# A graph layer on one core: where VectorE adds a block's sums to their bins

## The chip, the core and the metric

The kernel runs on one core of a Trainium2 chip. TensorE (PE; its weight loads are PEld), VectorE (DVE), ScalarE (ACT) and GpSimd (POOL) each work through a queue of their own; SyncE (SP) starts most transfers. The metric is the device time of one execution in microseconds (us). A measurement is the median of several runs; one execution more is taken with the hardware profiler, and all rows below are of it.

## The reference

A message-passing layer over 6250 nodes and 206250 edges, sorted by destination:

```python
msg = concat([x[col], edge_attr], axis=1)          # 64 + 64 columns
h = relu(msg @ W1a.T + b1a) @ W1b.T + b1b          # 128 hidden, 64 out
sums = segment_sum(h, row, num_segments=n_nodes)   # over the edges of a node
agg = sums / maximum(counts, 1.0)[:, None]
z = relu(concat([x, agg]) @ W2a.T + b2a) @ W2b.T + b2b
out = layernorm(x + concat([z, x]) @ Wr.T + br)
```

In `reference()` the node over which a message is summed (`row`) is the edge's `src`, and the features are gathered by `dst`. The edges are sorted by `dst`, so the gather is local and the sum is not.

## The kernel before

The edges come in tiles of 128, and 13 tiles make a block; there are 124 blocks (`NGR`). For each block the kernel makes the first layer's rows, finds for each row its place in a table in DRAM that is ordered by bins of 128 nodes, and scatters the rows there with GpSimd's indirect transfers. Once tiles of the table are full they are read back and summed into their bins by matmuls with one-hot matrices. The second layer is linear, so the sums are of first-layer rows (128 columns and a count), and the second layer comes after them.

Blocks 4 to 109 are *joined*: of their tiles six (nine in some early blocks) go another way. Four edges of a bin become one row group ("quad"), and TensorE does this by matmuls with marks. The order of work on TensorE, VectorE, ScalarE and SyncE is written by hand: it is the order of the program's text, in the loop at L1763. GpSimd's queue follows the data, and its scatters of one block are paced to the next one's matmuls.

What stands in a joined block k, in the order of the text:

- `marks(k, 0)` (L1246): VectorE compares two tiles' places with all quads (L1253, 1024 elements a partition); ScalarE does a third tile in two steps (L1258, L1259). `marks(k, 1)` comes later.
- `counts_of(k + 1)` (L1108 to L1121): TensorE counts the next block's rows by bin.
- `low_bits(k)` and `hidden(k, ...)` (L1374, L1376): the direct tiles' rows, TensorE at L1383, ScalarE's ReLU at L1387.
- `sum_first(k)` (L1633): the first half of a group of sums, TensorE at L1560, into a buffer of h_ps.
- `join_bases(k + 1)` (L1127, L1131): VectorE's next work behind the counts, then `join_ranks` on TensorE (L1140 to L1152), which waits for it.
- `bins_of`, `side`, `columns`: VectorE and ScalarE work for later blocks (L1059 to L1071, L1267 to L1274, L1336).
- In every second block from 10 to 58 `nodes_ahead` (L1723): the nodes' part of the second layer, TensorE at L1727 and L1729 into h_ps, copied to nx by VectorE (L1733).
- `slots`, `join_at_slots`, the last `hidden` part, then `join(k, 0)` and `join(k, 1)` (L1278): six matmuls each (L1285) into h_ps, copied to rj by ScalarE (L1290).
- `columns(k + 2, 1)` (L1338) and `join_places` (L1174 to L1185).
- `sum_rest(k, g)` (L1646): the group's second half on TensorE, then VectorE's one-hot matrices of the next group (`mark`, L1540), then `collect(1)` (L1620).
- `join_rows(k, i)` (L1292) for both joins: two groups each of two matmuls (L1298) into one h_ps, with ScalarE's ReLU to orow behind each (L1301).

`collect(n)` takes the oldest groups out of the list `totals` until n are left, and adds each one's h_ps to `part`, the bins' sums in SBUF. VectorE does this (L1631); where the bins hold nothing yet, ScalarE copies (L1629). In a joined block `collect(1)` stands behind `totals.append(g)`, so it takes the group of the block before and leaves the block's own one.

h_ps is one pool of PSUM buffers with `bufs=5` (L768). All the matmuls named above but counts and ranks write to it, and a buffer can be written again once its reader is through. The group of sums of block k holds one from `sum_first` in block k until it is collected.

Of the kernel before, what the change touches and what calls it, by code (L numbers as in the profile page):

```python
# [488 lines left out]
def fast_path(  # L489
# [64 lines left out]
    def joined(k):  # L554
        if not JOIN_FROM <= k < JOIN_TO:
            return 0
        return 3 if k in THRICE else 2
# [206 lines left out]
    with (  # L764
# [226 lines left out]
        def join_consts():  # L991
            for g in range(QUAD):
                nc.vector.tensor_scalar(
                    quad_ramp[:, g, :], ramp, float(QUAD), BIG + g, op0=ALU.mult, op1=ALU.add
                )
            nc.vector.memset(state["steps"], QSTRIDE + FULLQUADS)
            nc.vector.memset(state["steps"][:, :1], FULLQUADS)
# [248 lines left out]
        def marks(k, i):  # L1246


            m = top.marks[(join_at[k] + i) % MARKS]
            z = z_ps[:, i * JOIN : (i + 1) * JOIN]  # L1250
            all_q = quad_ramp.rearrange("p g q -> p (g q)")
            n = JOIN - ON_ACT
            nc.vector.tensor_tensor(  # L1253
                m[:, :n, :], all_q[:, None, :].to_broadcast([P, n, QUAD * P]),
                z[:, :n, None].to_broadcast([P, n, QUAD * P]), op=ALU.is_equal,
            )
            for t in range(n, JOIN):
                nc.scalar.activation(m[:, t, :], all_q, AF.Square, bias=z_acts[k][:, i * JOIN + t : i * JOIN + t + 1], scale=-1.0)  # L1258
                nc.scalar.activation(m[:, t, :], m[:, t, :], AF.Relu, bias=ones[:, :1], scale=-1.0)  # L1259
# [360 lines left out]
        def collect(n):  # L1620

            while len(totals) > n:
                g = totals.pop(0)
                to = part[:, g.b0 : g.b0 + g.nb, :]
                bins_ = range(g.b0, g.b0 + g.nb)
                assert len({b in begun for b in bins_}) == 1
                if g.b0 not in begun:
                    begun.update(range(g.b0, g.b0 + g.nb))
                    nc.scalar.copy(to, g.ps[:, : g.nb, :])  # L1629
                else:  # L1630
                    nc.vector.tensor_add(to, to, g.ps[:, : g.nb, :])  # L1631
# [131 lines left out]
        for k, ep_ in enumerate(epoch_of):  # L1763
# [10 lines left out]
                carried(k + 2)  # L1774
            if joined(k):
                marks(k, 0)
            if k == 1:
                join_consts()
            if k == 0:
# [340 lines left out]
```

## Time and profile before

| | |
|---|---|
| median of 3 runs | 1961.84 us |
| lowest and highest | 1957.87 and 1968.04 us |
| profiled execution | 1968.19 us, of which the span of the instructions is 1966.4 us |
| granted TensorE clock, mean | 0.914 |
| sums added by VectorE (L1631) | 192, 81.2 us in all |
| sums copied by ScalarE (L1629) | 25, median 0.375 us, from 483.5 to 825.1 us |

Rows of the timeline and of the waits look like this: start in us, duration in us, engine, line, operation, `out<-in` by the program's names, count; and in square brackets the idle time of the engine ahead of it and what ended it. `remote` is a releaser that the profile can't name, `issue` a wait for nothing that it shows. In a list of waits stand the engine and line that waited, what for, and us in total, times, longest us. In a list of groups stand busy us and mean ns of one, then the idle time ahead of them in us with its releasers. TensorE's matmuls in float32 are recorded as two halves. The ends of matmuls are modelled.

### The profile page before, as it was taken

The numbers are of one execution on the slowest core, as the hardware profiler recorded it, in microseconds if no ns is written. First come the engines' busy times: TensorE is split into PE (matmuls) and PEld (weight loads), VectorE is DVE, ScalarE is ACT, GpSimd is POOL, SyncE is SP. The second block draws the span as 40 slices with busy tenths as digits, with TensorE's granted clock in tenths as the row PEclk, the third lists the DMA queues.
The fourth block names the chain that finished last, engine by engine and source line by source line (L and its number), as shares of the span: only waits on it lengthen the run. The fifth ranks groups of instructions, "written<-read, shape, count | busy, mean of one in ns | idle before, by whom it ended". The sixth has DMA issues, their size and how long they took to land.

```text
span 1966.4 us, 33425 instructions
## 1 busy us (share of the span) xinstructions
PE 1576.4 (80%) x10868; PEld 1390.9 (71%) x10868; DVE 1355.3 (69%) x2959; ACT 1116.3 (57%) x2300; POOL 1153.7 (59%) x1235
## 2 busy tenths in 40 slices
PE   5477888768888878888888788888888888888597
PEld 4356666656777767777777677767777788887596
DVE  5367777777766766777767677777777767665287
ACT  2157778766666666666766666666666633222007
POOL 5555666566665665666666666666665656666501
PEclk7678989989998999999999989999989999999699
DMA  6546676656676666756666555556565789896484
GB/s 171 155 152 204 224 226 226 225 175 210 189 218 188 193 202 199 207 168 205 180 202 191 173 167 172 182 158 196 172 198 174 209 249 270 270 276 216 115 266 113
DMA packets 248791, 387.59 MB, mean 197 GB/s; under 512 B 43573, under 2 KB 181687, under 8 KB 248607
## 3 DMA queue, kind: packets, MB, share of 16 engines
q1 hardware_dynamic: 167661, 221.23, 40.4%
q0 software_dynamic: 48048, 122.08, 17.7%
q10 hardware_dynamic: 32898, 42.05, 6.4%
q8 instruction: 89, 1.46, 0.3%
q14 instruction: 95, 0.78, 0.1%
HBM read 214.47 MB, written 170.72 MB: 196 GB/s over the span
## 4 chain that ended last, share of the span: by engine, by line
PE 51%; ACT 13%; issue 11%; DVE 10%; another core or an unknown queue 10%; DMA 3%; POOL 1%; ACTq 0%; SPq 0%; DVEq 0%; POOLq 0%
PE h_ps L1560 19%; PE h_ps L1285 10%; PE h_ps L1298 8%; PE h_ps L1383 7%; DVE marks L1253 2%; ACT marks L1258 2%; ACT orow L1387 2%; DMA rows<-orow,rowidx 2%; ACT orow L1301 2%; ACT rj L1290 1%; ACT marks L1259 1%; ACT rhs L1336 1%; DVE oh L1540 1%; POOL rows L1427 1%
## 5 line engine op out<-in xcount | busy, mean ns | idle before, releaser
L1427 POOL DMA_INDIRECT rows<-orow,rowidx x949 | 926.5, 976 | 615.8 <-issue 215.1
L1560 PE MATMUL h_ps<-rt,oh 128*128 128x129 f32 x3952 | 532.5, 287 | 85.8 <-issue 66.4
L1560 PEld LDWEIGHTS h_ps<-rt,oh 128*128 128x128 f32 x3952 | 502.3, 201 | 116.3 <-issue 89.5
L1285 PE MATMUL h_ps<-marks,side 128*128 128x512 f32 x1326 | 362.0, 420 | 42.7 <-DVE nx L1733 34.4
L1387 ACT ACTIVATE orow<-h_ps 128x384 f32<-128x384 f32 (+1 forms) x275 | 146.9, 538 | 427.8 <-remote 162.4
L1298 PE MATMUL h_ps<-mv,rj 128*128 128x130 f32 x1768 | 268.7, 301 | 144.6 <-ACT rj L1290 71.6
L1298 PEld LDWEIGHTS h_ps<-mv,rj 128*128 128x128 f32 x1768 | 234.7, 206 | 181.3 <-ACT rj L1290 84.5
L1285 PEld LDWEIGHTS h_ps<-marks,side 128*128 128x128 f32 x1326 | 254.4, 200 | 100.7 <-DVE nx L1733 40.6
L1540 DVE TENSOR_TENSOR oh<-ramp,rt 128x768 f32<-128x768 bf16 (+4 forms) x391 | 308.6, 824 | 14.2 <-issue 9.5
L1383 PE MATMUL h_ps<-mv,rhs 124*128 124x128 f32 x1898 | 291.6, 300 | 19.5 <-issue 13.4
L1383 PEld LDWEIGHTS h_ps<-mv,rhs 124*128 124x128 f32 x1898 | 255.5, 208 | 26.3 <-issue 18.5
L1395 POOL DMA_INDIRECT rows<-orow,qidx x221 | 214.6, 971 | 95.8 <-issue 42.3
L1253 DVE TENSOR_TENSOR marks<-quad_ramp,ramp 128x1024 fp32r<-128x1024 f32 x221 | 265.5, 1205 | 0.0
L1301 ACT ACTIVATE orow<-h_ps 128x260 f32<-128x260 f32 x442 | 151.6, 388 | 117.6 <-PE h_ps L1298 47.3
L1290 ACT COPY rj<-h_ps 128x512 f32<-128x512 f32 x221 | 123.2, 588 | 157.3 <-remote 59.2
L1127 DVE TENSOR_SCALAR of_quads<-cnt_ps 128x98 bf16<-128x98 f32 x106 | 28.1, 265 | 217.7 <-PE cnt_ps L1117 114.4
L1259 ACT ACTIVATE marks<-marks,ones 128x512 fp32r<-128x512 f32 x221 | 159.7, 723 | 7.2
L1631 DVE TENSOR_TENSOR part<-part,h_ps 128x258 f32<-128x258 f32 (+2 forms) x192 | 81.2, 423 | 117.5 <-remote 64.5
L1258 ACT ACTIVATE marks<-quad_ramp,z_act 128x512 fp32r<-128x512 f32 x221 | 158.2, 716 | 0.0
L1212 DVE TENSOR_REDUCE row<-cnt_ps 128x7 f32<-128x350 f32 (+1 forms) x124 | 68.1, 549 | 106.4 <-remote 59.7
L1071 DVE TENSOR_TENSOR_SCAN had<-ramp,bins 128x400 bf16<-128x400 bf16 (+1 forms) x124 | 131.3, 1059 | 14.3 <-ACT orow L1301 1.1
L1336 ACT ACTIVATE rhs<-rhs,from_win 60x896 f32<-60x896 bf16 (+1 forms) x116 | 126.7, 1092 | 2.8
(194 smaller groups left out, 1566.0 us busy)
## 6 DMA issues: line engine op xcount, KB each, us to landing
rt<-rows SPq DMA_DIRECT2D x194, 390.0 KB
rt<-rows SPq DMA_DIRECT2D x97, 325.0 KB
rows<-padrow ACTq DMA_DIRECT2D x24, 1040.0 KB
rhs<-in_edgeT SPq DMA_DIRECT2D x97, 224.0 KB
enat<-in_edgeJ SPq DMA_DIRECT2D x97, 192.0 KB
rows<-orow,rowidx POOLq DMA_INDIRECT x949
rt<-rows SPq DMA_DIRECT2D x40, 260.0 KB
rhs<-relt SPq DMA_DIRECT2D x93, 105.0 KB
```

Of the source, the lines that this page charges most:

```text
L1253: nc.vector.tensor_tensor(m[:, :n, :], all_q[:, None, :].to_broadcast([P, n, QUAD * P]), z[:, :n, None].to_broadcast([P, n, QUAD * P]), op ...
L1258: nc.scalar.activation(m[:, t, :], all_q, AF.Square, bias=z_acts[k][:, i * JOIN + t : i * JOIN + t + 1], scale=-1.0)
L1259: nc.scalar.activation(m[:, t, :], m[:, t, :], AF.Relu, bias=ones[:, :1], scale=-1.0)
L1285: done[k, f"turn{i}"] = nc.tensor.matmul(ps, s[:, p, i * JOIN + t, :], m[:, t, :], start=t + p == 0, stop=t == JOIN - 1 and p == 1,).ins.name
L1298: done[k, f"join{i}"] = nc.tensor.matmul(ps[:, j, :], rj[:, (g0 + j) * P : (g0 + j + 1) * P], m, start=True, stop=True).ins.name
L1301: nc.scalar.activation(mrow[:, g0 : g0 + 2, :], ps, AF.Relu)
L1383: done[k, c] = nc.tensor.matmul(ps[:, j, :], rhs[:WIDE, of * P : (of + 1) * P], m[:WIDE, :H], start=True, stop=True).ins.name
L1387: nc.scalar.activation(orow_of(k, k0, n)[:, :, :H], ps[:, :n, :], AF.Relu)
L1395: s = nc.gpsimd.indirect_dma_start(out=qep.rows.rearrange("(q r) f -> q (r f)", r=QUAD), out_offset=bass.IndirectOffsetOnAxis(ap=qidx[:, q ...
L1427: s = nc.gpsimd.indirect_dma_start(out=ep_.rows, out_offset=bass.IndirectOffsetOnAxis(ap=rowidx[:, k % RING * BLK + j : k % RING * BLK + j ...
L1540: nc.vector.tensor_tensor(res[:, at_tile : at_tile + nb * n, :], ramp[:, None, :].to_broadcast([P, nb * n, P]), node[:, :, None].to_broadc ...
L1560: m = nc.tensor.matmul(of_bin(b), oh[:, at, :], rows, start=i == 0, stop=i == len(of) - 1)
```

## The change

In a joined block `collect(0)` is called right behind `marks(k, 0)`: the group that the block before left in `totals` is added to its bins there. By then `totals` has no other one. `collect(1)` in `sum_rest` stays, and in a joined block whose list is empty before it, it finds only the block's own group and leaves it.

```diff
             if joined(k):
                 marks(k, 0)
+                collect(0)
             if k == 1:
                 join_consts()
```

## The prediction

> **What bounds the kernel now.** I read the page first: where the busy time lies, and which engine the last chain runs through.
>
> ```profile
> span 1966.4 us, 33425 instructions
> PE 1576.4 (80%) x10868; PEld 1390.9 (71%) x10868; DVE 1355.3 (69%) x2959; ACT 1116.3 (57%) x2300; POOL 1153.7 (59%) x1235
> PE 51%; ACT 13%; issue 11%; DVE 10%; another core or an unknown queue 10%; DMA 3%; POOL 1%; ACTq 0%; SPq 0%; DVEq 0%; POOLq 0%
> ```
>
> No engine is full. TensorE is busy for 80% and carries half of the chain, so the time goes down where TensorE's waits in a block get shorter, and VectorE's own load (69%) matters only where TensorE waits for it. The second view is therefore TensorE's waits, in the two stages in which sums run in joined blocks: 470 to 830 us, where the bins are first copied, and 830 to 1560 us.
>
> ```profile
> PE h_ps L1285 <- DVE nx L1733: 33.7, 11, 4.0
> ...
> PE h_ps L1298 <- issue: 44.6, 48, 3.3
> PE h_ps L1298 <- ACT rj L1290: 29.1, 24, 6.5
> PE h_ps L1560 <- issue: 17.3, 28, 1.3
> PE h_ps L1298 <- ACT orow L1301: 10.9, 18, 1.0
> ```
>
> The first line is of the earlier stage, the others of the later one. The first and the last are no data dependences: a joining matmul (L1285) doesn't read nx, and the rows' matmuls (L1298) don't read orow. They wait because h_ps has five buffers and the next one is still being read. The other waits of L1298 on rj are real data. So the question is how many of the five buffers a sum holds, and that is what the change touches. The third view is the timeline of one block of each stage. First the later stage:
>
> ```profile
> 903.46 0.58 ACT L1290 COPY rj<-h_ps 128x512 f32<-128x512 f32 x1
> 904.09 1.16 PE L1298 MATMUL h_ps<-mv,rj 128*128 128x130 f32 x8 [0.21 <-issue]
> 904.85 1.81 DVE L1540 TENSOR_TENSOR oh<-ramp,rt 128x768 f32<-128x768 bf16 x2
> 906.58 0.41 DVE L1631 TENSOR_TENSOR part<-part,h_ps 128x258 f32<-128x258 f32 x1
> 906.91 1.21 DVE L1253 TENSOR_TENSOR marks<-quad_ramp,ramp 128x1024 fp32r<-128x1024 f32 x1
> 907.02 0.59 ACT L1290 COPY rj<-h_ps 128x512 f32<-128x512 f32 x1 [2.99 <-remote]
> 907.63 1.04 ACT L1338 ACTIVATE rhs<-rhs,ones 60x896 f32<-60x896 f32 x1
> 907.66 0.71 PE L1298 MATMUL h_ps<-mv,rj 128*128 128x130 f32 x4 [2.41 <-ACT rj L1290]
> 908.70 0.94 ACT L1301 ACTIVATE orow<-h_ps 128x260 f32<-128x260 f32 x3
> 909.14 1.24 PE L1298 MATMUL h_ps<-mv,rj 128*128 128x130 f32 x4 [0.76 <-ACT orow L1301]
> 910.41 0.39 ACT L1301 ACTIVATE orow<-h_ps 128x260 f32<-128x260 f32 x1 [0.77 <-PE h_ps L1298]
> 911.32 0.26 DVE L1127 TENSOR_SCALAR of_quads<-cnt_ps 128x98 bf16<-128x98 f32 x1 [3.20 <-PE h_ps L1298]
> ```
>
> A block's joined rows take four buffers, one for each group of four L1298 (two halves of two matmuls). The fourth starts at 909.14, 0.05 us after the first ReLU could be done (908.70, and 0.39 for one), though its rj was there since 907.61. It has to reuse the first group's buffer. ScalarE then waits 0.77 us for it, and VectorE's next step, L1127, has waited 3.20 us for what TensorE does behind it. So this wait is on the path at the seam of two blocks.
>
> Counting buffers says why. In the tail of block k two of five are held by sums: that of block k-1, until the add L1631 at 906.58 to 906.99, and that of block k itself. Three are left for four groups. The add does end before 909.14, but at the place in the order where the buffers are dealt out its buffer comes late in the row; the wait on the ReLU shows that it isn't the one taken.
>
> Then a block of the earlier stage, in which nodes_ahead takes a buffer too:
>
> ```profile
> 527.96 1.68 PE L1285 MATMUL h_ps<-marks,side 128*128 128x512 f32 x6
> 532.94 0.56 DVE L1733 COPY nx<-h_ps 128x384 f32<-128x384 f32 x1 [3.42 <-remote]
> 533.02 0.49 ACT L1387 ACTIVATE orow<-h_ps 128x384 f32<-128x384 f32 x1 [2.93 <-remote]
> 533.41 0.58 ACT L1290 COPY rj<-h_ps 128x512 f32<-128x512 f32 x1
> 533.56 2.93 PE L1285 MATMUL h_ps<-marks,side 128*128 128x512 f32 x6 [3.92 <-DVE nx L1733]
> 535.75 1.82 DVE L1540 TENSOR_TENSOR oh<-ramp,rt 128x768 f32<-128x768 bf16 x2
> 537.48 1.21 DVE L1253 TENSOR_TENSOR marks<-quad_ramp,ramp 128x1024 fp32r<-128x1024 f32 x1
> 537.95 1.95 PE L1298 MATMUL h_ps<-mv,rj 128*128 128x130 f32 x16
> 538.18 0.38 ACT L1629 COPY part<-h_ps 128x258 f32<-128x258 f32 x1
> 540.41 0.26 DVE L1127 TENSOR_SCALAR of_quads<-cnt_ps 128x98 bf16<-128x98 f32 x1 [1.72 <-PE cnt_ps L1117]
> ```
>
> Here old sum, new sum, nodes_ahead, the last hidden group and the first join hold all five, and the second join stands for 3.92 us until nx is copied. That copy itself was held up by 3.42 us: TensorE's results become visible to VectorE and ScalarE at the same moment, 532.94 and 533.02, long after it issued them. What holds them no row says; I leave it in place.
>
> **The change, part by part.** In a joined block the sum left over from block k-1 is added (or, the first time, copied) right behind the first marks, instead of behind the two oh of block k's sum_rest. No instruction is added or removed: the same adds, copies, matmuls and DMAs. SP's order and the issue points stay, POOL's too. The later collect in sum_rest finds nothing left to do.
>
> *The moved add.* Its rows, with those of the step that comes behind it:
>
> ```profile
> L1631 DVE TENSOR_TENSOR part<-part,h_ps 128x258 f32<-128x258 f32 (+1 forms) x63 | 25.8, 410 | 0.0
> L1127 DVE TENSOR_SCALAR of_quads<-cnt_ps 128x98 bf16<-128x98 f32 x77 | 20.1, 261 | 125.4 <-PE cnt_ps L1117 82.4 <-PE h_ps L1298 19.0 <-remote 16.4
> ```
>
> One add is 0.41 us. It now stands between marks and L1127, which waits 125.4 us in 77 blocks, 1.6 us each; this wait hides the add, and the marks start 0.41 us sooner. Cost zero; where L1127 doesn't wait it would be 0.41 a block (the rival below). The add itself waits for the old sum's matmuls, which precede the rows in TensorE's order, so it is ready at once; where a block has a second sum, these matmuls come just ahead of the counts for which L1127 waits anyway.
>
> *The moved copy.* The 0.38 us copy (L1629) leaves the place between L1338 and the ReLUs and goes behind the marks' ScalarE part. ScalarE waits later in that block (2.93 us at 533.02), so it costs nothing there. Taken at zero; with 25 such copies in the trace it can't bring more than 25 x 0.38 = 9.5 us.
>
> *The freed buffer, earlier stage.* The second join no longer needs nx's buffer. In the block shown it can start at 529.64, when the first ends, and then the old sum's successor and the rows follow as soon as rj is there (533.99). TensorE would be done with the rows 3.8 us sooner. But VectorE isn't: from nx at 532.94 its chain runs as before to the end of marks, 538.69, then comes the add to 539.1, and only there can L1127 start, against 540.41. So 1.3 us arrive (1.72 less 0.41). With 11 such waits that is 14 us. The bounds are 0 and the whole wait of 33.7.
>
> *The freed buffer, later stage.* With one sum held instead of two, four buffers are there for four groups, and the fourth group starts behind the third. That frees 0.76 us of TensorE in the block shown. In other blocks the same wait is booked under another name:
>
> ```profile
> 893.61 0.94 ACT L1301 ACTIVATE orow<-h_ps 128x260 f32<-128x260 f32 x3
> 894.05 0.71 PE L1298 MATMUL h_ps<-mv,rj 128*128 128x130 f32 x4 [0.76 <-ACT rhs L1338]
> 894.80 0.39 ACT L1301 ACTIVATE orow<-h_ps 128x260 f32<-128x260 f32 x1 [0.25 <-issue]
> ```
>
> Again TensorE starts just as the first ReLU ends (893.61 and 0.39 is 894.00), but here ScalarE loses only 0.25 us. So the 18 waits named after orow are the floor, 10.9 us, and most of the 48 put down to "issue" are of this kind; 10.9 + 44.6 = 55.5 is the ceiling. The stage has some 53 blocks (730 us by 13.8). I take one wait a block, of which between 0.25 (ScalarE's loss) and 0.76 (TensorE's) reaches the next block, so 0.5: 26 us. I cut this to 22, since some blocks have no such wait, and keep 0 and 40 (53 x 0.76) as ends.
>
> *The sum.* 14 + 22 = 36 us. The profiled execution took 1968.2 us (span 1966.4), so 1932 for it; the median of the runs is 1961.8, a factor of 0.9968, which makes **1926 us**.
>
> [...]
>
> **The rivals.**
>
> *The wait only changes its name (no change, 1953 to 1966 us).* TensorE gets to its next wait sooner and stands there instead: at rj (29.1 us now), or at the late release seen in the 2.99 and 3.42 us "remote" waits. If the moment of that release is set by the transfers of the block and not by TensorE's progress, the time freed in front of it is lost. Against it: the fourth group stands behind that release, not in front of it, and L1127's wait shows TensorE late at the seam. For it: that is just what holds in the earlier stage. Less than 9 us would then be left: 1953 or more.
>
> *The buffer isn't used where it is missing (no change, 1962 us).* Which buffer an h_ps takes is settled when the program is built, and the trace doesn't show it. If the order gives the early one to a step that never waited, the fourth group still reuses the first's. By the count of five this needs an order that passes over a free buffer, as it does today with the one of the add.
>
> *Everything goes through (1888 us).* All of 33.7, and 53 x 0.76 = 40: 74 us off the profiled time, scaled.
>
> *The add in front of L1127 is paid (slower, 1975 us).* VectorE works through its queue in order. Of the 77 L1127, the waits of the view cover some 55; in 22 blocks it starts without waiting, so VectorE is what is late, and 0.41 us in front delays the ranks for which TensorE waits: 22 x 0.41 = 9 us now. It gets worse if blocks shorten at TensorE's end and VectorE becomes the bound in all 77: 32 us. It decides if L1127's wait falls below 0.41 us in most blocks without the buffers bringing anything: 9 to 32 us over 1962, in the middle of the lower half 1975. Against it stands the mean wait of 1.6 us. [...] The rows of VectorE above run in the order of the code.
>
> **How the numbers follow.** Forecast 0.60 (1926; its own range 1900 to 1951), everything goes through 0.12, the wait changes its name 0.13, buffer not used 0.08, add is paid 0.07. A measurement of this kernel can't tell less than about 0.5% (10 us) from no change. Faster by more than that: 0.60 + 0.12 = 0.72. Same: 0.13 + 0.08 = 0.21. Slower: 0.07. For the range I leave out the slower case and the lower half of "everything goes through", together 0.13, and a little of the forecast's lower edge: 1893 to 1964.
>
> **What would show it.** The line "PE h_ps L1285 <- DVE nx L1733" should be gone or below 5 us, and "PE h_ps L1298 <- ACT orow L1301" with it. The four ReLUs L1301 should run without a break before the fourth. In the timeline L1631 should follow the first L1253 of a block, and L1127's wait should shrink by about what the blocks gain, but not vanish. Blocks of 830 to 1540 us should take about 0.4 us less each. It is wrong if these waits go and the waits on rj, or "remote" ones, grow by as much; if the orow wait stays; or if L1127 starts right behind L1631 in most blocks.

## The result and the profile after

| | before | after |
|---|---|---|
| median of 6 runs | 1966.32 us | 1944.32 us |
| lowest and highest | 1957.87 and 1973.78 us | 1940.60 and 1954.08 us |
| profiled execution | 1968.19 us | 1942.51 us |

The ratio is 0.9887, 95% interval 0.9855 to 0.9918: faster by 22 us, where 36 were forecast. The page of the changed kernel, with its span, the busy time of the engines and the shares of the last chain:

```profile
span 1940.7 us, 33425 instructions
...
PE 1579.9 (81%) x10868; PEld 1385.6 (71%) x10868; DVE 1354.7 (70%) x2959; ACT 1106.2 (57%) x2300; POOL 1156.6 (60%) x1235
...
PE 50%; DVE 15%; ACT 11%; another core or an unknown queue 10%; issue 10%; DMA 2%; POOL 1%; ACTq 1%; DVEq 0%; SPq 0%; POOLq 0%
```

The same work, and VectorE now has 15% of the chain instead of 10%. TensorE's longest waits in the earlier stage, 470 to 830 us:

```profile
PE h_ps L1560 <- issue: 18.7, 39, 1.2
PE h_ps L1285 <- issue: 11.2, 24, 1.0
```

The 33.7 us of joins that waited for nx are gone; the whole list doesn't have that line. The same view of the later stage, 830 to 1560 us:

```profile
PE h_ps L1560 <- issue: 51.7, 107, 1.0
PE h_ps L1298 <- ACT rj L1290: 28.0, 31, 6.6
PE h_ps L1298 <- issue: 10.0, 11, 1.8
PE h_ps L1560 <- ACT orow L1301: 7.4, 6, 5.0
```

Here the rows' wait on orow (10.9) is gone, and "issue" fell from 44.6 to 10.0. The sums (L1560) took 34 us of it back: their "issue" was 17.3 us before. And 7.4 us of waits for the same ReLU, L1301, now stand at the sums, where the stage had none before. The timeline of a seam in this stage shows the new order:

```profile
894.18 1.21 DVE L1253 TENSOR_TENSOR marks<-quad_ramp,ramp 128x1024 fp32r<-128x1024 f32 x1
894.64 0.59 ACT L1290 COPY rj<-h_ps 128x512 f32<-128x512 f32 x1 [3.01 <-remote]
...
895.28 1.16 PE L1298 MATMUL h_ps<-mv,rj 128*128 128x130 f32 x8 [2.44 <-ACT rj L1290]
895.31 0.42 DVE L1631 TENSOR_TENSOR part<-part,h_ps 128x258 f32<-128x258 f32 x1
...
896.32 1.23 ACT L1301 ACTIVATE orow<-h_ps 128x260 f32<-128x260 f32 x4
...
897.06 0.26 DVE L1127 TENSOR_SCALAR of_quads<-cnt_ps 128x98 bf16<-128x98 f32 x1 [1.34 <-PE h_ps L1298]
...
905.23 0.52 DVE L1212 TENSOR_REDUCE row<-cnt_ps 128x7 f32<-128x350 f32 x1 [3.05 <-PE h_ps L1285]
905.31 0.49 ACT L1387 ACTIVATE orow<-h_ps 128x384 f32<-128x384 f32 x1 [2.57 <-PE h_ps L1285]
```

The add follows the marks, eight L1298 and four ReLUs run without a break, as forecast. But rj is still 3.01 us late, and 8 us further on VectorE and ScalarE stand together for 3.05 and 2.57 us and go on within 0.08 us of each other: the late release is still there.

Where did the freed time go? The groups of VectorE (busy us, mean ns | idle ahead of them), first before, from 470 to 1560 us, then after, from 470 to 1540 us, which holds as many blocks; L1127's line of before stands in the prediction:

```profile
L1212 DVE TENSOR_REDUCE row<-cnt_ps 128x7 f32<-128x350 f32 x78 | 40.7, 521 | 94.2 <-remote 52.6 <-PE h_ps L1285 41.5
L1733 DVE COPY nx<-h_ps 128x384 f32<-128x384 f32 (+1 forms) x14 | 7.6, 541 | 28.4 <-remote 25.4 <-PE h_ps L1285 3.0
```

```profile
L1212 DVE TENSOR_REDUCE row<-cnt_ps 128x7 f32<-128x350 f32 x78 | 40.8, 523 | 150.6 <-remote 131.9 <-PE h_ps L1285 18.7
L1631 DVE TENSOR_TENSOR part<-part,h_ps 128x258 f32<-128x258 f32 (+1 forms) x63 | 26.1, 415 | 21.9 <-PE h_ps L1383 16.4 <-remote 2.9 <-PE cnt_ps L1117 2.1
L1127 DVE TENSOR_SCALAR of_quads<-cnt_ps 128x98 bf16<-128x98 f32 x77 | 19.8, 257 | 25.9 <-remote 12.0 <-PE cnt_ps L1117 10.2 <-issue 2.2
L1733 DVE COPY nx<-h_ps 128x384 f32<-128x384 f32 (+1 forms) x14 | 7.6, 542 | 37.2 <-remote 18.6 <-PE h_ps L1285 18.6
```

L1127's wait at the seam fell by 125.4 - 25.9 = 99.5 us. Of that, 56.4 came back at L1212, 21.9 at the add itself and 8.8 at nx: 87 us went from one wait into others. By stages it is clearer. From 470 to 830 us L1127's wait fell from 29.0 to 9.9, and the waits of L1212, nx and the add together grew by only 7.3. From 830 to 1540 us L1127's fell from 96.3 to 16.0 us, by 80.3, and the others took 79.9 of it back: 56.7 at L1212, 20.3 at the add, 2.9 at nx. L1212 in that later stage, before and then after:

```profile
L1212 DVE TENSOR_REDUCE row<-cnt_ps 128x7 f32<-128x350 f32 x51 | 26.4, 518 | 61.7 <-remote 46.6 <-PE h_ps L1285 15.1
```

```profile
L1212 DVE TENSOR_REDUCE row<-cnt_ps 128x7 f32<-128x350 f32 (+1 forms) x52 | 27.4, 526 | 118.4 <-remote 104.5 <-PE h_ps L1285 13.9
```

One row a block lets the stages be timed. The first, the 56th and the last of the 106 L1127, before and then after:

```profile
77.89 0.25 DVE L1127 TENSOR_SCALAR of_quads<-cnt_ps 128x98 bf16<-128x98 f32 x1
...
842.36 0.26 DVE L1127 TENSOR_SCALAR of_quads<-cnt_ps 128x98 bf16<-128x98 f32 x1 [1.30 <-PE cnt_ps L1117]
...
1539.13 0.26 DVE L1127 TENSOR_SCALAR of_quads<-cnt_ps 128x98 bf16<-128x98 f32 x1 [0.51 <-PE cnt_ps L1117]
```

```profile
77.47 0.26 DVE L1127 TENSOR_SCALAR of_quads<-cnt_ps 128x98 bf16<-128x98 f32 x1
...
828.78 0.26 DVE L1127 TENSOR_SCALAR of_quads<-cnt_ps 128x98 bf16<-128x98 f32 x1 [0.83 <-PE cnt_ps L1117]
...
1518.22 0.26 DVE L1127 TENSOR_SCALAR of_quads<-cnt_ps 128x98 bf16<-128x98 f32 x1
```

Up to the 56th: 764.5 us, then 751.3, so 13.2 less. From there to the last: 696.8, then 689.4, so 7.3 less in 50 blocks, 0.15 each. With 0.4 us ahead of the first and 4.8 behind the last these are the 25.7 us by which the two spans differ. They are one execution of each kernel, and six executions of before lie 16 us apart, so the split is rough.

### The profile page after: what moved, and what is told of

Same layout as the page of the kernel before. It is cut to its first block, busy times and chain, and to the rows that moved or that the text cites. A ratio compares the mean times of both kernels' runs of the same rounds, so it can differ in the third digit from the quotient of the medians.

```text
span 1940.7 us, 33425 instructions
## 1 busy us (share of the span) xinstructions
PE 1579.9 (81%) x10868; PEld 1385.6 (71%) x10868; DVE 1354.7 (70%) x2959; ACT 1106.2 (57%) x2300; POOL 1156.6 (60%) x1235
## 4 chain that ended last, share of the span: by engine, by line
PE 50%; DVE 15%; ACT 11%; another core or an unknown queue 10%; issue 10%; DMA 2%; POOL 1%; ACTq 1%; DVEq 0%; SPq 0%; POOLq 0%
PE h_ps L1560 20%; PE h_ps L1285 8%; PE h_ps L1298 8%; PE h_ps L1383 7%; DVE marks L1253 3%; DVE oh L1540 2%; ACT marks L1258 2%; ACT rhs L1336 1%; ACT orow L1387 1%; ACT marks L1259 1%; DMA rows<-orow,rowidx 1%; ACT orow L1301 1%; ACT rj L1290 1%; PE cnt_ps L1117 1%
## 5 line engine op out<-in xcount | busy, mean ns | idle before, releaser
L1560 PE MATMUL h_ps<-rt,oh 128*128 128x129 f32 x3952 | 546.3, 286 | 134.1 <-issue 116.3
L1560 PEld LDWEIGHTS h_ps<-rt,oh 128*128 128x128 f32 x3952 | 497.9, 198 | 182.8 <-issue 157.6
L1387 ACT ACTIVATE orow<-h_ps 128x384 f32<-128x384 f32 (+1 forms) x275 | 146.4, 538 | 456.4 <-PE h_ps L1383 204.9
L1285 PE MATMUL h_ps<-marks,side 128*128 128x512 f32 x1326 | 356.9, 413 | 15.7 <-issue 14.1
L1298 PE MATMUL h_ps<-mv,rj 128*128 128x130 f32 x1768 | 259.5, 304 | 94.7 <-ACT rj L1290 64.3
L1298 PEld LDWEIGHTS h_ps<-mv,rj 128*128 128x128 f32 x1768 | 238.5, 213 | 119.8 <-ACT rj L1290 80.0
L1285 PEld LDWEIGHTS h_ps<-marks,side 128*128 128x128 f32 x1326 | 250.0, 197 | 75.8 <-issue 28.4
L1383 PE MATMUL h_ps<-mv,rhs 124*128 124x128 f32 x1898 | 287.2, 298 | 11.6 <-ACT orow L1301 5.1
L1395 POOL DMA_INDIRECT rows<-orow,qidx x221 | 214.2, 969 | 86.9 <-issue 33.6
L1383 PEld LDWEIGHTS h_ps<-mv,rhs 124*128 124x128 f32 x1898 | 251.6, 206 | 18.1 <-issue 9.3
L1301 ACT ACTIVATE orow<-h_ps 128x260 f32<-128x260 f32 x442 | 147.7, 389 | 137.0 <-PE h_ps L1298 53.1
L1212 DVE TENSOR_REDUCE row<-cnt_ps 128x7 f32<-128x350 f32 (+1 forms) x124 | 68.2, 550 | 161.3 <-remote 132.9
L1338 ACT ACTIVATE rhs<-rhs,ones 60x896 f32<-60x896 f32 (+1 forms) x116 | 126.4, 1090 | 2.9
```

The lines of the kernel that those rows point to most:

```text
L1285: done[k, f"turn{i}"] = nc.tensor.matmul(ps, s[:, p, i * JOIN + t, :], m[:, t, :], start=t + p == 0, stop=t == JOIN - 1 and p == 1,).ins.name
L1298: done[k, f"join{i}"] = nc.tensor.matmul(ps[:, j, :], rj[:, (g0 + j) * P : (g0 + j + 1) * P], m, start=True, stop=True).ins.name
L1301: nc.scalar.activation(mrow[:, g0 : g0 + 2, :], ps, AF.Relu)
L1383: done[k, c] = nc.tensor.matmul(ps[:, j, :], rhs[:WIDE, of * P : (of + 1) * P], m[:WIDE, :H], start=True, stop=True).ins.name
L1387: nc.scalar.activation(orow_of(k, k0, n)[:, :, :H], ps[:, :n, :], AF.Relu)
L1395: s = nc.gpsimd.indirect_dma_start(out=qep.rows.rearrange("(q r) f -> q (r f)", r=QUAD), out_offset=bass.IndirectOffsetOnAxis(ap=qidx[:, q ...
```

## The experiments

They ran on four chips, by the numbers in their results. On these the kernel before takes 1584 to 1587 us, not 1966. The result above names no chip; by its times it is taken here for that of another one. Each ratio below is against the kernel before on the same chip.

The first theory: the gain is the h_ps buffer that comes free earlier. Its rival: the gain is the order on VectorE, that the add no longer stands at the block's end.

**hold: early add, buffer held as before.**

```diff
             if joined(k):
                 marks(k, 0)
+                kept = list(totals)
                 collect(0)
...
+            for old in kept:
+                nc.vector.tensor_copy(seen, old.ps[:, 0, :1])
+            kept.clear()
```

The second part stands in `sum_rest`, behind the one-hot matrices.

> The changed kernel, and at the old place of the add (behind the two one-hot matrices of sum_rest) VectorE copies one element of a partition from the old group's h_ps into a tile that nobody reads. So the add stands early, but the buffer is held as long as before the change. Theory (the gain of 22 us is the buffer): the time is back at that of before, ratio 1.00 +- 0.003, the waits of the joins L1285 on nx (33.7 us in 11 before) and of the rows L1298 on orow L1301 (10.9 in 18) are back. Rival (the gain is the order of the add on VectorE, the buffer only happens to come free): the time stays at that of the changed kernel, 0.987 to 0.992, but for the 77 added copies, which by the shortest rows of VectorE on h_ps (0.41 us) are 77 x 0.3 = some 20 us of VectorE at most and are mostly hidden.

Measured: 1586.76 us, ratio 1.0006 (0.9993 to 1.0019). Of the two waits that should come back its trace has none on nx, and 7.4 us in 19 on orow L1301.

**ctl: the same copy from `part`.** `old.ps[:, 0, :1]` is replaced by `part[:, old.b0, :1]`.

> The control to hold: the same copy of one element at the same place, but from part in SBUF, so that h_ps is free after the early add. Both theories expect the time of the changed kernel, 0.987 to 0.993. If it is slower than that, the added copies themselves cost time, and hold must be read against this run: the buffer is worth the difference of the two.

Measured: 1587.31 us, 1.0003 (0.9993 to 1.0013).

**early and late: `collect(0)` under `if k < 60` or `if k >= 60`.**

> The early add only in blocks below 60, where the nodes' part of the second layer also takes a buffer; from block 60 on the add stands at its old place. By the prediction's own terms the earlier stage brings 14 us: ratio 0.993. By the block lengths of the two traces (13 + 13 joined blocks below 60 shortened by 9.6 and 6.9 us) it brings 16 us: 0.992. If the freed buffer of one block lengthened a later one, it would be 0.996 or more.

> The early add only from block 60 on. By the prediction's own term the later stage brings 22 us: ratio 0.989. By the block lengths of the two traces it brings 0.14 us in each of 44 blocks and 1.7 in the tail, 8 us: 0.996. If the first theory holds (time freed in the later stage runs into the late release of TensorE's results) the rows' waits of TensorE on orow are gone here as in the changed kernel, and ScalarE's waits on the hidden rows (L1387 on L1383) are longer.

Measured: early 1586.77 us, 1.0001 (0.9992 to 1.0010); late 1586.27 us, 1.0001 (0.9990 to 1.0012).

The three kernels expected below 1 by the buffer, ctl, early and late, missed. Four kernels with one time tell nothing of buffer or order; they tell that on this chip neither is worth anything. So the unaltered change had to be run there.

**again: the changed kernel.** **hold_again: hold once more.**

> The changed kernel, unaltered, once more. The four kernels before this one ran on a chip on which the kernel before the change takes 1587 us instead of 1966, and all of them took the same 1587. Theory (the buffer is worth something only where TensorE's results reach the other engines late, as in the two first traces): on a chip with 1587 us before, ratio 1.000 +- 0.002; on one with some 1960 us before, 0.989 +- 0.004. Rival (the change brings 1% anywhere, and the four edits each lost it): 0.989 on either.

> The changed kernel with the buffer held to the old place by the copy of one element. On a chip with some 1960 us before: theory (the gain is the buffer) ratio 1.000 +- 0.004, rival (the gain is the order of the add on VectorE) 0.989. On a chip with 1587 us before it shows nothing new: 1.000.

Measured: 1584.37 us, 0.9997 (0.9983 to 1.0011), and 1585.41 us, 1.0008 (0.9992 to 1.0025). The change brings nothing on such a chip. Its trace says what is different there; the groups of VectorE from 380 to 1235 us, which hold about the same blocks as the table above:

```profile
L1212 DVE TENSOR_REDUCE row<-cnt_ps 128x7 f32<-128x350 f32 x75 | 38.5, 513 | 0.0
...
L1733 DVE COPY nx<-h_ps 128x384 f32<-128x384 f32 (+1 forms) x13 | 7.0, 535 | 0.0
```

The work takes as long (513 and 535 ns an instruction, against 523 and 542 in after), but nothing waits for a late release: 0.0 us instead of 150.6 and 37.2.

Does the freed buffer do nothing there? The three L1127 rows of hold_again, then of again, both on one chip:

```profile
44.37 0.25 DVE L1127 TENSOR_SCALAR of_quads<-cnt_ps 128x98 bf16<-128x98 f32 x1
...
677.62 0.25 DVE L1127 TENSOR_SCALAR of_quads<-cnt_ps 128x98 bf16<-128x98 f32 x1
...
1233.70 0.25 DVE L1127 TENSOR_SCALAR of_quads<-cnt_ps 128x98 bf16<-128x98 f32 x1
```

```profile
45.63 0.26 DVE L1127 TENSOR_SCALAR of_quads<-cnt_ps 128x98 bf16<-128x98 f32 x1
...
659.25 0.25 DVE L1127 TENSOR_SCALAR of_quads<-cnt_ps 128x98 bf16<-128x98 f32 x1
...
1234.53 0.25 DVE L1127 TENSOR_SCALAR of_quads<-cnt_ps 128x98 bf16<-128x98 f32 x1
```

It does: with the buffer freed, the first half takes 613.6 us instead of 633.2. (On another chip ctl and early, which free it too, take 615.0 and 613.2; hold takes 629.2, and late, where the add itself stands late until block 60, 620.5.) Then 575.3 instead of 556.1: of the 19.6 us 19.2 are given back. ScalarE's waits say to whom. From 470 to 830 us hold_again has no wait of L1374 on a transfer; again has this one:

```profile
ACT orow L1374 <- DMA rows<-orow,rowidx: 28.9, 12, 4.5
```

L1374 writes into orow, and by this row it stood 28.9 us in all for GpSimd's scatters, which read the old rows there. The scatters of again in the whole span:

```profile
L1427 POOL DMA_INDIRECT rows<-orow,rowidx x949 | 926.9, 977 | 298.3 <-issue 139.5 <-DMA rows<-orow,rowidx 26.4 <-PE h_ps L1298 17.1
L1395 POOL DMA_INDIRECT rows<-orow,qidx x221 | 219.5, 993 | 67.4 <-issue 18.9 <-ACT orow L1301 8.8 <-DMA rows<-orow,rowidx 8.2
```

Busy and idle, 1170 scatters take 926.9 + 298.3 + 219.5 + 67.4 = 1512 us of 1587, one each 1.29 us. The idle 0.3 us ahead of each I count as part of the scatter and not as slack, for it is the same whatever the row names for its end:

```profile
605.78 0.97 POOL L1427 DMA_INDIRECT rows<-orow,rowidx  x1 [0.30 <-ACT rj L1290]
607.06 0.97 POOL L1427 DMA_INDIRECT rows<-orow,rowidx  x1 [0.30 <-PE h_ps L1298]
```

In again 1167 of the 1170 are between 0.30 and 0.32 us. In the first trace none is below 0.30 either, but 287 are above 0.32: there the same scatters have 711.6 us of idle time (615.8 and 95.8) instead of 365.7. So in again GpSimd goes from one scatter to the next without a break, and in the first trace it doesn't.

This gives a second theory in two parts. Where results are on time, GpSimd's scatters are the bound and a buffer on TensorE is worth nothing. Where results come late, blocks are longer than the scatters, and buffers run short. Both parts were tried.

**lag_before, lag_after, lag_hold: late readers put in.** Before, after and hold each get:

```diff
+        def delay():
+            for _ in range(5):
+                nc.scalar.copy(dly, padrow[:, :512])
...
             rj = turned[k, i] = top.rjs[(join_at[k] + i) % 2]
+            if i == 1 and k not in nodes_at:
+                delay()
             nc.scalar.copy(rj, ps)
...
+            delay()
+            nc.vector.tensor_copy(dly_seen, dly[:, :1])
             nc.vector.tensor_copy(top.nx[:, : n * (P + D)], ps[:, : n * (P + D)])
```

> The kernel before the change, with late readers put in: in each block with joins ScalarE does five idle copies of 128x512 (5 x 0.59 = 3 us) ahead of the copy of join 1 to rj; in a block with nodes_ahead they stand ahead of nx instead, and VectorE's copy to nx waits for them. This imitates the 2.99 and 3.42 us for which the readers stood in the first trace. On a chip with 1587 us before it should take some 100 x 1.5 to 3 us more, 1740 to 1890 us. Theory (late readers make h_ps short): the trace shows the waits of L1285 on nx and of L1298 on orow L1301 that the first trace had, with over 10 us in each stage. Rival: they stay at the 7 us in 8 and the 6 in 16 that the traces of the chips with 1587 us show.

> The changed kernel with the same late readers. Theory (the freed buffer is worth something where readers are late): 10 to 30 us below lag_before, a ratio of 0.985 to 0.995 between the two, and the waits on nx and orow L1301 gone. Rival (the gain of the first runs is of another kind than late readers): the same time as lag_before within 0.2%.

> The changed kernel with late readers, and the buffer of the last block's sums held to the old place by the copy of one element. Theory (buffer): the time of lag_before within 0.3%. Rival (order of the add on VectorE): that of lag_after.

| | median, us | ratio to before | interval |
|---|---|---|---|
| lag_before | 1803.42 | 1.1392 | 1.1363 to 1.1421 |
| lag_after | 1765.31 | 1.1145 | 1.1118 to 1.1172 |
| lag_hold | 1826.74 | 1.1536 | 1.1506 to 1.1566 |

With late readers the change brings 38 us, 1.1145/1.1392 = 0.978 (0.973 to 0.983 by the ends of the intervals). That is more than the 10 to 30 us expected. With the buffer held it brings nothing, though the add stands early. So it is the buffer, not the order; the 77 added copies are 11.5 us in lag_hold's trace, and 1826.7 less all of these is 1815 us, still above lag_before. TensorE's waits of lag_before (L1287, L1302, L1391 and L1633 are L1285, L1298, L1387 and L1629 of before):

```profile
PE h_ps L1302 <- ACT rj L1294: 186.8, 113, 7.9
PE h_ps L1287 <- ACT orow L1391: 33.6, 13, 4.0
...
PE h_ps L1302 <- ACT part L1633: 8.8, 12, 0.7
```

The joins wait again for a buffer, 33.6 us in 13 as against 34.4 in 12 in the first trace's whole span; here the ReLU is named, whose reading is what was delayed. In lag_after this line is gone, in lag_hold it is back with 36.0 us (below). The rows' wait on orow L1301 (L1305 here), of which over 10 us in the later stage were expected, is not in the list: the imitation has the earlier stage's shortage and not the later one's. Nor is it a copy of the earlier: by the L1127 of single blocks, from the 31st to the 56th, 11.6 of 14.7 us were saved in blocks with nodes_ahead in the first traces, while with late readers these got 7.5 us longer and the blocks between them 40.9 us shorter. lag_hold missed by more than its 0.3%: it is 23 us above lag_before. Its waits have the joins' line again, and name the held buffer:

```profile
PE h_ps L1287 <- ACT orow L1391: 36.0, 13, 4.0
PE h_ps L1302 <- DVE seen L1663: 31.9, 10, 5.2
```

In blocks where ScalarE copied the old sums, VectorE's copy behind the one-hot matrices releases them still later than ScalarE did: 31.9 less the 8.8 above is 23.1 us, about the excess, though a sum of waits need not arrive in full: of the 99.5 us by which L1127's wait fell in the first traces, some 20 did. The L1127 rows (L1129 here) of lag_before and of lag_after:

```profile
44.84 0.26 DVE L1129 TENSOR_SCALAR of_quads<-cnt_ps 128x98 bf16<-128x98 f32 x1
...
819.11 0.26 DVE L1129 TENSOR_SCALAR of_quads<-cnt_ps 128x98 bf16<-128x98 f32 x1 [0.91 <-PE cnt_ps L1119]
...
1459.30 0.26 DVE L1129 TENSOR_SCALAR of_quads<-cnt_ps 128x98 bf16<-128x98 f32 x1 [3.62 <-PE cnt_ps L1119]
```

```profile
45.50 0.25 DVE L1129 TENSOR_SCALAR of_quads<-cnt_ps 128x98 bf16<-128x98 f32 x1
...
787.13 0.26 DVE L1129 TENSOR_SCALAR of_quads<-cnt_ps 128x98 bf16<-128x98 f32 x1 [0.29 <-PE cnt_ps L1119]
...
1423.20 0.26 DVE L1129 TENSOR_SCALAR of_quads<-cnt_ps 128x98 bf16<-128x98 f32 x1
```

774.3 to 741.6 us in the first half, 640.2 to 636.1 in the second: 32.7 and 4.1, the earlier stage first, as in the two traces at the top.

**lag_late: lag_after with `collect(0)` under `if k >= 60`.**

> With the late readers of lag_before, the early add only from block 60 on. lag_before took 1.139 of the time before, lag_after 1.1145, so the change brings 38 us there. By the block lengths of the two traces 33 us of it come from the blocks 24 to 58 and 5 from the later ones: ratio 1.136 +- 0.003. By the prediction's terms (14 earlier, 22 later) 23 of the 38 would come from the later blocks: 1.125.

Measured: 1803.87 us, 1.1380 (1.1357 to 1.1404), where lag_before has 1.1392. Nearly all of the 38 us come from the blocks below 60. As the imitation has no shortage in the later stage, this says nothing of the 22 us that the prediction had for it.

**more_pool: a memset of 0.5 us for GpSimd written into each joined block of the changed kernel.** **more_act: 0.6 us more on ScalarE,** the delay of lag_after with `range(1)`. The edit of more_pool, ahead of a block's last scatter:

```diff
+                if joined(k) and j == BLK - 1:
+                    nc.gpsimd.memset(idle, 0.0)
                 t = k * BLK + j
```

> The changed kernel, and in each of the 106 joined blocks one idle memset of 128x512 on GpSimd ahead of the block's last scatter (0.52 us by the row of the memset of 128x520). Theory: on the chips with 1587 us GpSimd is the bound, it issues one scatter each 1.28 us without a break, and what TensorE gains is lost again in ScalarE's wait for the scatters (L1374). Then all of it arrives: 106 x 0.5 = 55 us, or up to 87 if the 0.3 us between two instructions come on top; ratio 1.03 to 1.055. Rival (TensorE is the bound there, as the chain says): under 10 us, 1.000 to 1.006.

> The changed kernel, and in the same 106 blocks one idle copy of 128x512 on ScalarE (0.59 us) ahead of the copy of join 1, that is, one fifth of what lag_after has. TensorE waits for that copy. Theory (GpSimd is the bound): TensorE's own slack takes it, under 15 us, ratio 1.000 to 1.009. Rival (TensorE is the bound): 106 x 0.59 = 63 us, or half of it where the next sums cover it: 1.02 to 1.04.

Measured: more_pool 1635.63 us, 1.0327 (1.0308 to 1.0346); more_act 1593.19 us, 1.0054 (1.0038 to 1.0069). The added group in more_pool's trace:

```profile
L1428 POOL MEMSET idle<- 128x512 f32 x106 | 56.6, 534 | 5.5
```

Of its 56.6 us, 51.6 arrive (1635.63 - 1584.01), a little under the bound expected. But this isn't the test that was meant. The memset waits for no data, and the trace doesn't have one in each block: 20 of the 106 ran before 37 us, all by 156 us, and many in rows like this one:

```profile
81.48 19.17 POOL L1428 MEMSET idle<- 128x512 f32 x33
```

So more_pool stalls GpSimd in the first blocks, and that the total fits 0.5 us a block is luck. What it shows is that GpSimd doesn't make up lost time. Against again, which ran on another chip, the L1127 rows (L1128 here) come 36.1 us later at the 14th (193.78 and 157.65) and 48.9 at the last (1283.39 and 1234.53), with no memset in between. The 36.1 us don't tell which is the bound, for a stall of 19 us in one row may hold up the other engines in either case; that they lose another 13 us without one fits a GpSimd without slack.

The copies of more_act do stand in their blocks, from 78 to 1261 us. Of ScalarE's 106 x 0.59 = 63 us ahead of a copy for which TensorE waits, 9 arrive. This speaks against TensorE as the bound on these chips. That GpSimd is rests on the scatters without a break, on the time given back in again and on the time not made up here; no run has 0.5 us in each block. The chain of again doesn't name it:

```profile
PE 47%; DMA 19%; ACT 16%; DVE 9%; issue 5%; POOL 1%; SPq 1%; ACTq 1%; DVEq 0%; POOLq 0%
```

## Why the prediction was right, and where it wasn't

The direction and the range (1893 to 1964) held: 1944.32 us, against 1926. So did the mechanism, the buffer that comes free, but in the later stage most of its gain was lost at the next wait. With the larger term three times too high, the range of 71 us held by its width. By its steps:

- **The freed buffer, earlier stage: 14 us.** Right, as far as one execution of each kernel can tell. The line on nx is gone, and the blocks up to the 56th take 13.2 us less. From the 31st to the 56th, 12 blocks with nodes_ahead take 11.6 us less, about 1 us each where 1.3 was forecast. That it is the buffer is shown by lag_hold, with imitated lateness; on the chip of the first traces itself hold wasn't run.
- **The freed buffer, later stage: 22 us.** The step that failed, by its size: 7.3 us came. The waits went as foretold (10.9 to none, 44.6 to 10.0). Wrong was "between 0.25 (ScalarE's loss) and 0.76 (TensorE's) reaches the next block, so 0.5": 0.15 did. L1212's wait grew instead, by 56.7 us in that stage.
- **"The fourth group stands behind that release, not in front of it"**, the argument against the rival of the changed name. It overlooked the next release: what the fourth group gains is time in front of the following block's, and there it was lost. In the later stage this rival was right in the main, in the earlier one the forecast; what sets the moment of the release isn't shown. L1212 and nx were rows to ask of before: they waited for "remote" 52.6 and 25.4 us.
- **The moved add at zero, "ready at once".** It isn't: 63 adds wait 21.9 us in all. L1127's wait, now 0.34 us in the mean, is below the 0.41 us of the add, the point that the slower rival named. Its other half, that the buffers bring nothing, didn't come true.
- **"What holds them no row says; I leave it in place."** The size of the result hangs on this. Where results come on time, the ratio of the same change is 0.9997. The prediction held for the chip of its profile and said nothing of another.
- **What would show it.** The four ReLUs, the add behind the marks, and the gone lines are as written. "0.4 us less each" in the later blocks isn't, and L1127's wait didn't shrink "by about what the blocks gain" but by 99.5 us for some 20. Of its signs of being wrong, growing "remote" waits came: L1212's went from 52.6 to 131.9 us.

So one more free buffer for TensorE's groups was worth 13.2 us in the earlier stage of the first traces and 32.7 with imitated lateness; on the chip of again, where the scatters leave GpSimd no break, it was worth 0.0% (ratio 0.9997).

## What to carry to other kernels

A wait for a free buffer is worth what lies behind it: before counting it, look for the next wait in the same block that ends at a moment of its own, and put down only what gets past it (here 45.5 us of L1298's waits went in the later stage, and 7.3 us of time). When two traces of one kernel differ, look for the engine with the least slack in each; an idle instruction on it, and one on its rival, help to tell which is the bound where the chain names another, but look in the trace where they ran: one that waits for nothing may run long before its place (more_pool's 106 memsets had all run by 156 us). A gain of 1% is a gain on the chip of the profile until it has been run on a second: 0.9887 here, 0.9997 there.

## What the runs showed of the hardware

The kernel takes 1966 us in the first runs and 1584 to 1587 in the later ones on four chips, with the same work: VectorE is busy for 1355.3 us in before and for 1345.1 in again, and q1's packets take 40.4% of 1966.4 us, 794, in before and 49.5% of 1585.0, 785, in hold. TensorE's busy time, whose ends are modelled, is longer: 1576.4 us in before and 1430.8 in again. What differs besides is when TensorE's results reach their readers: in the first trace L1212 and nx wait for them, 94.2 and 28.4 us between 470 and 1560 us, in again 0.0 us between 380 and 1235. GpSimd's scatters come each 1.29 us there without a break. The granted clock is 0.914 and 0.924 in the first two traces, 0.967 to 0.976 in the runs of hold. The lower clock needn't be the cause: on a chip where before has 0.965 to 0.976, lag_before, with its added waits, has 0.936 to 0.941. What makes the results late stays open, and so does whether it is the chip or its state at that time: no later run of before took 1966 us again, so hold wasn't tried under these conditions.
